# Residual input of the first three projection tiles loaded during the last attention head, into the convolution's buffers

## The chip, the cores and the metric

The kernel runs on one core of a Trainium2 chip. The metric is the device time of one execution in microseconds (us), as the median of several runs; the profile comes from one further execution, taken by the hardware profiler.

## The reference

The input `x` is 1 x 48 x 256 x 256 in float32. Two layers follow, each of the form x + f(group norm of x):

```
# layer 0: attention over 4x4 patches
qkv  = dwconv3x3(einsum('bchw,oc->bohw', gn(x), w_qkv), w_dw)     # 3 x 48 channels
q, k, v = 8 heads of (96, patches); 64 x 64 patches (+ a border of padding)
attn = softmax(normalise(q)^T normalise(k) * temperature)
out  = fold(v attn)                                                # back to 48 x 256 x 256
x    = x + einsum('bchw,oc->bohw', out, w_proj)
# layer 1: three separable mixings of 64 x 64 windows
x    = x + sum_t einsum('bcphqw,wW,hH,cC->bCpHqW', gn(x), Ws[t], Hs[t], Cs[t])
```

The step `x + einsum(out, w_proj)` between the attention and layer 1 is called the projection here; the `x` in it is the residual input.

## The kernel before

The program runs in five stages: statistics and the first pointwise convolution (to 138 us), the depthwise convolution of head 0, eight heads of attention (from 290 us), the projection (3233 to 3385 us) and layer 1.

**Attention.** The loop over heads `h` and sixteen groups `g` of two query blocks is written out by hand under a manual schedule, so instructions stand on each engine in the order of the code. A group runs `scores` (line L337 on TensorE, the exponential L566 on ScalarE), `normalised`, and four calls of `weigh` (`k` = 0 to 3, L595 on TensorE, added up by VectorE in L606 into `oacc`). Queries for group `g + 2` are loaded by SP (L311) as soon as `scores` has read the queries of group `g`, since there are two `qt` buffers. Between these steps heads 0 to 6 also carry the convolution for the head after: strips of the pointwise convolution and the rows of `Depthwise`. Their tiles live in the pool `cv` (`ots`, `xs`, `pad`, `acc`, `o`, `oh` and others), which is opened ahead of the attention and closed with it. In the last head (`more` is false) there is no convolution, and `cv` is not used any more.

**End of a head.** `store(h, m)` turns 512 columns of `oacc` with four transposes (L612), copies them on ScalarE into `oo` (L614, two buffers) and has POOL send them to `os__70` in DRAM as two DMAs (L616). In the last group the stores for `m` = 0 to 5 come at `k` = 1 to 3, and those for `m` = 6 and 7 after the loop.

**Projection.** Eight tiles of 96 partitions (two halves of 48 channels) and 16 rows each. For a tile, SP loads the attention's output `pot` (L740) and the residual input `pxt` (L741), a half at a time, 768 KB a half. TensorE multiplies `pot` by `wp` in four steps (L746, three PSUM buffers), VectorE adds each to `pxt` in place (L753) and takes statistics (L757, eight a tile), and POOL stores the sum to `x1s` in DRAM (L762). The pool `pj` has three buffers each for `pot` and `pxt`; a buffer of `pot` is free when TensorE has read it, one of `pxt` when its store to `x1s` has landed. Here the order on each engine is chosen by the tile scheduler; the order on SP begins with both halves of the first `pxt`, then three of `pot`, then `pxt` and `pot` in turn.

```
ot = pj.tile([P2, KK, NP], F32, name="pot")
xt = pj.tile([P2, RP, W], F32, name="pxt")
for s in range(2):
    ...
    nc.sync.dma_start(out=ot[r], in_=ov[s * (NT // 2 // TP) + t])
    nc.sync.dma_start(out=xt[r], in_=xc[:, y0 : y0 + RP, :])
```

Layer 1 starts when all statistics are there and `x1s` is written: SP loads `lxq` from it (L815).

DMAs of SP and of POOL each rotate over eight semaphores, so the ninth of an engine's DMAs waits for the first one's end.

Of the kernel before, what the change touches and what calls it, by code (L numbers as in the profile page):

```python
# [8 lines left out]
F32 = mybir.dt.float32  # L9
# [7 lines left out]
C = 48  # L17
H = W = 256
HALF = H // 2
P2 = 2 * C  # L20
KS = 4
KK = KS * KS
NH = 8
HD = C * KK // NH
# [9 lines left out]
PX = W // KS  # L34
# [5 lines left out]
TP = 256  # L40
# [5 lines left out]
def conv_preact_kernel(  # L46
# [15 lines left out]
    nc = tc.nc  # L62
    xc = x.rearrange("b c y x -> (b c) y x")
# [34 lines left out]
    for s in range(2):  # L98
        r = slice(s * C, (s + 1) * C)
        for h in range(NH if s == 0 else H0):  # L100
            o = s * M0 + h * HC if h < H0 else (h - H0) * HC
            nc.gpsimd.dma_start(
                out=(wq[r] if h < H0 else wr[0:C])[:, o : o + HC].rearrange("c (z e) -> c z e", z=3),
                in_=w_qkvT.rearrange("c (z h e) -> h c z e", z=3, h=NH)[h],
# [198 lines left out]
    NM = NT // 512  # L303
# [99 lines left out]
    with tc.tile_pool(name="xn", bufs=1) as xnp, tc.tile_pool(name="cst", bufs=1) as cst, tc.tile_pool(  # L403
        name="nps", bufs=2, space=PSUM
# [9 lines left out]
        for i, LR in enumerate(parts):  # L414
            j = sum(parts[:i])
            for s in range(2):
                eng = nc.sync if s == 0 else nc.scalar
                eng.dma_start(
                    out=xr[s * C : (s + 1) * C, j : j + LR, :], in_=xc[:, s * HALF + j : s * HALF + j + LR, :]
# [8 lines left out]
        for g, (w, k) in enumerate(((wq, P2), (wr, C))):  # L428
            m = w.shape[1]
# [48 lines left out]
                nc.sync.dma_start(out=rows, in_=ot[s * M0 : (s + 1) * M0])  # L478

    attention = ExitStack()  # L480
    cv = attention.enter_context(tc.tile_pool(name="cv", bufs=1))
    one = attention.enter_context(tc.tile_pool(name="one", bufs=2, space=PSUM))

    ots = [cv.tile([M1, 4, W + 2], F32, name=f"ot{i}") for i in range(NOT)]
# [5 lines left out]
    with tc.If(nc.values_load(large) > 0):  # L490
# [8 lines left out]
        with tc.tile_pool(name="mk", bufs=NM) as mk, tc.tile_pool(name="mq", bufs=2) as mq, tc.tile_pool(  # L499
            name="mps", bufs=2, space=PSUM  # L500
# [23 lines left out]
    with tc.tile_pool(name="ahead", bufs=2) as ah, tc.tile_pool(name="ae", bufs=3) as ae, tc.tile_pool(  # L524
        name="asm", bufs=6
    ) as asm, tc.tile_pool(name="ao", bufs=1) as ao, tc.tile_pool(name="big", bufs=3, space=PSUM) as big:
        MB = 8
        NK = NB // MB
        NG = NB // G
        keys, queries, values, oaccs = {}, {}, {}, {}  # L530

# [76 lines left out]
        def store(h, m):  # L608

            pt = one.tile([HD, 4, 128], F32, name="pt", tag="one")  # L610
            for i in range(4):
                nc.tensor.transpose(pt[:, i, :], oaccs[h, m // 2][:, m % 2, i * HD : (i + 1) * HD], ident)  # L612
            oo = asm.tile([HD, 512], F32, name="oo", bufs=2)
            nc.scalar.copy(oo, pt.rearrange("p i n -> p (i n)"))  # L614
            for i in range(512 // TP):
                nc.gpsimd.dma_start(  # L616
                    out=os_[m * (512 // TP) + i, h * HD : (h + 1) * HD, :], in_=oo[:, i * TP : (i + 1) * TP]
                )
# [16 lines left out]
        with tc.manual_schedule():  # L635
            load_query(0, 1)
            block = scores(0, 0)
            for h in range(NH):
                more = h + 1 < NH
                rows = {r: Depthwise(h + 1, r) for r in range(CR + 1)} if more else {}  # L640
                for g in range(NG):
                    p, d, n = rows.get(g - 2), rows.get(g - 1), rows.get(g)

                    if h == 0 and 0 < g <= 6:
                        load_value(0, g + 1)
                    if more and CR + 2 <= g < CR + 6:
                        for m in range(2):
                            load_value(h + 1, (g - CR - 2) * 2 + m)
                    if more and CR + 3 <= g < CR + 6:
                        for m in range(2):  # L650
                            load_key(h + 1, (g - CR - 3) * 2 + m)

                    blocks = [normalised(*block)]
                    if p:
                        p.norm()
                        p.root()
                    block = scores(h, g * G + 1)
                    if more and g == NG - 1:
                        load_key(h + 1, 6)
                        load_key(h + 1, 7, nc.gpsimd)  # L660
                    if g + 2 < NG:
                        load_query(h, g + 2)
                    elif more:
                        load_query(h + 1, g + 2 - NG)
                    if p:
                        p.scale()
                    if d:
                        for t in range(1, 4):
                            d.tap(t)
                    second = block  # L670
                    if g + 1 < NG:
                        block = scores(h, (g + 1) * G)
                    elif more:
                        block = scores(h + 1, 0)
                    blocks.append(normalised(*second))
                    if d:
                        for t in range(4, 9):
                            d.tap(t)

                    if g == 0 and rows:  # L680
                        rows[0].load()

                    if h == 0 and 0 < g <= 6:
                        turn(0, g + 1)
                    if more and CR + 2 <= g < CR + 6:
                        for m in range(2):
                            turn(h + 1, (g - CR - 2) * 2 + m)
                    if g == 0 and h > 0:
                        for m in range(6, 8):
                            store(h - 1, m)  # L690
                    if p:
                        p.patches()
                        p.store((2,))
                        p.high()
                    if d:
                        d.square()
                    if n:
                        n.first()
                    for k in range(NK):
                        s = (h * NG + g) * NK + k  # L700
                        weigh(h, g, blocks, k)
                        if k == 0 and d:
                            d.reduce()
                        if k == 0 and p:
                            p.low(nc.gpsimd)
                            p.store((0, 1))
                        if s % 2:
                            for w in strips[s - 1] + strips[s]:
                                w.run(big.tile([128, 2, 512], F32, name="big"))
                            for w in strips[s + 1] + strips[s + 2]:  # L710
                                w.load()
                        elif s:
                            for w in strips[s - 2] + strips[s - 1]:
                                w.store()
                        if k == 2 and g + 1 in rows:
                            rows[g + 1].load()

                        if g == NG - 1 and k > 0:
                            for m in range(2 * k - 2, 2 * k):
                                store(h, m)  # L720
            for m in range(6, 8):
                store(NH - 1, m)
# [1 line left out]


    l1c = ctx.enter_context(tc.tile_pool(name="l1c", bufs=1))
    RP = TP // PX * KS
    NP = TP
    with tc.tile_pool(name="pj", bufs=3) as pj, tc.tile_pool(name="pjs", bufs=1) as pjs, tc.tile_pool(
        name="pps", bufs=3, space=PSUM  # L730
# [2 lines left out]
        ov = os_.rearrange("t (c k) n -> t c k n", k=KK)  # L733
        for t in range(HALF // RP):
            ot = pj.tile([P2, KK, NP], F32, name="pot")
            xt = pj.tile([P2, RP, W], F32, name="pxt")
            for s in range(2):
                r = slice(s * C, (s + 1) * C)
                y0 = s * HALF + t * RP
                nc.sync.dma_start(out=ot[r], in_=ov[s * (NT // 2 // TP) + t])  # L740
                nc.sync.dma_start(out=xt[r], in_=xc[:, y0 : y0 + RP, :])  # L741
            xv = xt.rearrange("p (py ki) (px kj) -> p ki kj py px", ki=KS, kj=KS)
            for ki in range(KS):
                ps = pps.tile([P2, KS, NP], F32, name="pps")
                for i in range(0, KS, 2):
                    nc.tensor.matmul(  # L746
                        ps[:, i : i + 2, :],
                        lhsT=wp,
                        rhs=ot[:, ki * KS + i : ki * KS + i + 2, :],
                        start=True,  # L750
                        stop=True,
                    )
                nc.vector.tensor_add(  # L753
                    xv[:, ki], ps.rearrange("p k (py px) -> p k py px", py=RP // KS), xv[:, ki]
                )
            for i in range(0, RP, 2):
                nc.vector.bn_stats(  # L757
                    st1[:, (t * RP + i) // 2, :], xt[:, i : i + 2, :].rearrange("p a b -> p (a b)")
                )
            for s in range(2):  # L760
                y0 = s * HALF + t * RP
                nc.gpsimd.dma_start(out=x1s[:, y0 : y0 + RP, :], in_=xt[s * C : (s + 1) * C])  # L762
# [14 lines left out]
        for s in range(2):  # L777
            nc.scalar.dma_start(
                out=csn[s * 64 : s * 64 + C].rearrange("c (t d) -> c t d", t=T3), in_=Cs.rearrange("t c d -> c t d")
            )  # L780
            r = slice(s * 64, s * 64 + C)
# [4 lines left out]
        nc.tensor.matmul(pb1, lhsT=mrow, rhs=csn[0:C], start=True, stop=True)  # L786
        cbias = l1c.tile([128, T3 * C], F32, name="cbias")
        nc.vector.tensor_copy(cbias, pb1)


    with tc.tile_pool(name="lx", bufs=3) as lx, tc.tile_pool(name="lz", bufs=2) as lz, tc.tile_pool(
        name="lr", bufs=2
# [109 lines left out]
        with tc.manual_schedule():  # L902
# [4 lines left out]
            late = None  # L907
# [57 lines left out]
```

## Time and profile before

| | us |
|---|---|
| median of 3 runs | 3701.59 |
| lowest, highest | 3696.06, 3705.06 |
| profiled execution, its time | 3698.24 |
| profiled execution, its span | 3696.2 |
| last head's last score matmul ends | 3207.7 |
| first projection matmul (L746) | 3238.9 |
| last statistics of the projection (L757) end | 3379.9 |
| first load of layer 1 (L815) issued | 3384.7 |

The span is the stretch from the first to the last instruction of the profiled execution; what lies around it makes its time 2.0 us longer. The page divides the span into 40 slices of 92.4 us and gives a digit for each engine's busy tenths. Waits name the engine and line that waited, what ended the wait, then the sum in us, the count and the longest. A table of stretches has the busy time of each engine, the granted TensorE clock, the mean busy share of the sixteen DMA engines (1.00 is all of them busy) and the GB/s they moved.

### The profile page before, as it was taken

How to read it: one execution, taken by the hardware profiler on the slowest of the kernel's cores; microseconds unless marked ns; L12 is line 12 of the kernel's file. 1: busy time of each engine (PE TensorE's matmuls, PEld its weight loads, DVE VectorE, ACT ScalarE, POOL GpSimd, SP SyncE). 2: the span in 40 equal slices, each digit the busy share in tenths (PEclk: the TensorE clock that was granted, in tenths of full speed). 3: DMA queues.
4: the chain of work that ended last, by engine and by line, in shares of the span. 5: the costliest groups of instructions: out<-in, count | busy, mean ns of one | idle time of the engine just before them, and what ended most of it. 6: DMA issues, size and time to landing. Idle time of an engine off the chain costs nothing.

```text
span 3696.2 us, 100318 instructions
## 1 busy us (share of the span) xinstructions
PE 3466.8 (94%) x44252; PEld 2905.8 (79%) x44252; DVE 2139.4 (58%) x3514; ACT 1873.3 (51%) x2747; POOL 542.9 (15%) x628
## 2 busy tenths in 40 slices
PE   2869999999999999999999999999999999855998
PEld 1337777898888898988888989888889888713776
DVE  5454774189628953894399349925982222266654
ACT  0235676566546654665566556655664444300332
POOL 2030111012111211121122112201220000000011
PEclk9989999999999999999999999999999999966999
DMA  7455666533323332333233323332333100299774
GB/s 160 152 133 153 176 170 171 149 96 95 94 79 82 93 89 75 83 90 96 73 92 86 87 73 93 86 87 84 94 79 87 36 19 19 51 248 197 127 138 92
DMA packets 274146, 386.48 MB, mean 105 GB/s; under 512 B 77010, under 2 KB 211522, under 8 KB 269480
## 3 DMA queue, kind: packets, MB, share of 16 engines
q1 hardware_dynamic: 234790, 264.95, 27.4%
q0 software_dynamic: 35424, 106.40, 12.4%
q10 hardware_dynamic: 3490, 8.64, 1.1%
q8 instruction: 350, 5.73, 0.7%
q14 instruction: 92, 0.75, 0.1%
HBM read 234.76 MB, written 144.90 MB: 103 GB/s over the span
## 4 chain that ended last, share of the span: by engine, by line
PE 82%; DMA 6%; DVE 2%; issue 1%; SPq 1%; ACT 1%; ACTq 0%; POOL 0%; POOLq 0%; DVEq 0%
PE big L337 36%; PE big L595 35%; PE pb L863 4%; PE pa L841 2%; PE pc L880 2%; DMA pxt<-in_x_dram 2%; DMA t<-ot 1%; PE big L177 1%; DVE acc L228 1%; PE pt L612 1%; DMA pad<-t 1%; PE pn L247 1%; DMA pot<-os__70 1%; PE pst L549 1%; DMA x1s<-pxt 0%
## 5 line engine op out<-in xcount | busy, mean ns | idle before, releaser
L566 ACT ACTIVATE e<-big,nmx 128x1024 f32<-128x1024 f32 x1024 | 1143.8, 1118 | 875.5 <-PE big L337 613.1
L337 PE MATMUL big<-kt,qt 128*128 128x512 f32 x6144 | 1436.7, 392 | 31.1 <-DMA kt<-qkv 29.0
L595 PEld LDWEIGHTS big<-vn,e 128*64 128x64 f32 x32768 | 1357.0, 137 | 57.2 <-ACT e L566 30.6
L595 PE MATMUL big<-vn,e 128*64 128x96 f32 x32768 | 1387.3, 247 | 6.1 <-DVE oacc L606 2.5
L337 PEld LDWEIGHTS big<-kt,qt 128*128 128x128 f32 x6144 | 1144.6, 188 | 279.6 <-issue 28.8
L606 DVE TENSOR_TENSOR oacc<-big,oacc 128x768 f32<-128x768 f32 x480 | 453.4, 954 | 713.0 <-PE big L595 713.0
L228 DVE SCALAR_TENSOR_TENSOR acc<-pad,dwt,acc 126x1024 f32<-126x1024 f32 x592 | 765.5, 1293 | 39.8 <-ACT acc L209 24.0
L295 POOL DMA_DIRECT2D qkv<-o x72 | 52.8, 734 | 1240.7 <-ACT o L279 1240.7
L579 DVE TENSOR_REDUCE zt<-zs 128x1 f32<-128x4 f32 x256 | 38.4, 150 | 335.1 <-ACT e L566 335.1
L289 POOL TENSOR_TENSOR ol<-o,oh 126x1024 fp32r<-126x1024 f32 x78 | 184.9, 2370 | 311.1 <-DVE ss L243 237.8
L566 ACT ACTIVATION_READ_ACCUMULATOR e<-big,nmx 128x1 f32 x1024 | 196.3, 192 | 0.0
L848 DVE TENSOR_TENSOR lzt<-pa,cbias 128x864 f32<-128x864 f32 (+1 forms) x88 | 137.0, 1628 | 96.4 <-PE pa L841 96.4
L870 ACT COPY lyt<-pb 128x512 f32<-128x512 f32 x144 | 84.5, 587 | 212.4 <-PE pb L863 212.4
L279 ACT COPY o<-acc 126x1024 f32<-126x1024 f32 x74 | 159.1, 2150 | 0.0
L863 PEld LDWEIGHTS pb<-wsb,lzt 128*64 128x64 f32 x2304 | 126.1, 138 | 27.6 <-issue 19.5
L616 POOL DMA_DIRECT2D os__70<-oo x128 | 65.2, 515 | 541.6 <-ACT oo L614 541.3
L863 PE MATMUL pb<-wsb,lzt 128*64 128x128 f32 x2304 | 142.0, 279 | 1.3 <-issue 1.3
L746 PE MATMUL pps<-pot,wp 96*96 96x512 f32 x128 | 79.1, 787 | 61.5 <-DMA pot<-os__70 61.5
L239 ACT ACTIVATE sq<-acc 126x1024 f32<-126x1024 f32 x74 | 78.2, 1057 | 100.7 <-DVE acc L228 100.7
L180 ACT ACTIVATE ot<-big,bias 108x1024 f32<-108x1024 f32 x64 | 68.2, 1111 | 113.1 <-PE big L177 71.4
L209 ACT ACTIVATE acc<-pad,dwt 126x1024 f32<-126x1024 f32 x74 | 84.1, 1137 | 80.6 <-DMA pad<-t 80.6
L746 PEld LDWEIGHTS pps<-pot,wp 96*96 96x96 f32 x128 | 26.9, 219 | 113.3 <-issue 79.0
(124 smaller groups left out, 1977.0 us busy)
## 6 DMA issues: line engine op xcount, KB each, us to landing
pad<-t SPq DMA_DIRECT2D x238, 254.0 KB
t<-ot SPq DMA_DIRECT2D x128, 217.7 KB
qkv<-ol POOLq DMA_DIRECT2D x78, 336.0 KB, 6.1
qkv<-oh POOLq DMA_DIRECT2D x70, 336.0 KB, 5.6
qt<-qkv SPq DMA_DIRECT2D x176, 96.0 KB
xs<-in_x_dram SPq DMA_DIRECT2D x128, 96.0 KB
os__70<-oo POOLq DMA_DIRECT2D x128, 96.0 KB, 2.1
pxt<-in_x_dram SPq DMA_DIRECT2D x16, 768.0 KB
```

The costliest lines, as they stand in the source:

```text
L209: nc.scalar.mul(self.acc, self.pad[:, 0:KS, 0:W], dwt[:, self.h, 0:1])
L228: nc.vector.scalar_tensor_tensor(self.acc, self.pad[:, dy : dy + KS, dx : dx + W], dwt[:, self.h, tap : tap + 1], self.acc, ALU.mult, ALU.add,
L279: nc.scalar.copy(self.o.rearrange("p (a b) x -> p a b x", a=KS), self.acc.rearrange("p a (x b) -> p a b x", b=KS))
L289: eng.tensor_sub(self.ol, self.o, self.oh.bitcast(F32))
L337: nc.tensor.matmul(ps[:, i, :], lhsT=qt[:, r, q0 : q0 + 128], rhs=kts[2 * j + i][:, r // 2, :], start=(r == 0), stop=(r == 2),)
L566: nc.scalar.activation(e[:, j * 1024 : (j + 1) * 1024], ps.rearrange("p a b -> p (a b)"), AF.Exp, bias=nmx[:, b : b + 1], accum_out=zs[:, ...
L595: nc.tensor.matmul(ps[p : p + 64, j // 4, j % 4 * HD : (j % 4 + 1) * HD], lhsT=e[:, mb * 128 + p : mb * 128 + p + 64], rhs=vn, start=(i == 0),
L606: nc.vector.tensor_add(oaccs[h, k], ps[:, :, : 4 * HD], oaccs[h, k])
L746: nc.tensor.matmul(ps[:, i : i + 2, :], lhsT=wp, rhs=ot[:, ki * KS + i : ki * KS + i + 2, :], start=True, stop=True,)
L848: nc.vector.tensor_tensor(zv[:, :, y0 : y0 + n, :], pa[:, :, : n * T3 * C].rearrange("p s (y k) -> p s y k", y=n), cbias.rearrange("p (u v ...
L863: nc.tensor.matmul(pb[s * WS : (s + 1) * WS, i, :], lhsT=zts[u][:, t * C + c + i, :], rhs=wsb[:, t, :], start=True, stop=True,)
L870: nc.scalar.copy(yt[:, t, :], pb.rearrange("p i x -> p (i x)"))
```

## The change

The pool `cv` gets a stack of its own at the other end of the on-chip memory (`side="right"`). At the start of the last head it is closed, and a pool `pe` takes its place with three tiles `xt0` to `xt2` for the residual input of projection tiles 0 to 2, and with one `oo` buffer for the very last store (`m` = 7). In groups 1 to 6 of the last head SP gets four loads a group, each a quarter of a half (48 partitions, 4 rows, 192 KB): two at `k` = 1 and two at `k` = 3. The projection uses these tiles for `t` < 3 and issues loads of `pxt` for the other five alone. With `cv` gone from the low end, the pools of the attention and `pj` move down there.

```diff
     attention = ExitStack()
-    cv = attention.enter_context(tc.tile_pool(name="cv", bufs=1))
+    convolution = ExitStack()
+    cv = convolution.enter_context(tc.tile_pool(name="cv", bufs=1, side="right"))
+    NX = 3
     one = attention.enter_context(tc.tile_pool(name="one", bufs=2, space=PSUM))
...
         NK = NB // MB
+        NLATE = 1
+        RP = TP // PX * KS
...
-            oo = asm.tile([HD, 512], F32, name="oo", bufs=2)
+            late = h == NH - 1 and m >= NM - NLATE
+            oo = (pe if late else asm).tile([HD, 512], F32, name="oo", bufs=NLATE if late else 2)
...
                 for g in range(NG):
                     p, d, n = rows.get(g - 2), rows.get(g - 1), rows.get(g)
 
+                    if not more and g == 0:
+                        convolution.close()
+                        early = ExitStack()
+                        pe = early.enter_context(tc.tile_pool(name="pe", bufs=1, side="right"))
+                        xts = [pe.tile([P2, RP, W], F32, name=f"xt{t}") for t in range(NX)]
...
                         if k == 2 and g + 1 in rows:
                             rows[g + 1].load()
+                        if not more and 0 < g <= 2 * NX and k in (1, 3):
+                            i = (g - 1) * 2 + k // 2
+                            t, y = i // 4, i % 4 * (RP // 4)
+                            for half in range(2):
+                                y0 = half * HALF + t * RP + y
+                                nc.sync.dma_start(
+                                    out=xts[t][half * C : (half + 1) * C, y : y + RP // 4, :],
+                                    in_=xc[:, y0 : y0 + RP // 4, :],
+                                )
...
-    RP = TP // PX * KS
...
-            xt = pj.tile([P2, RP, W], F32, name="pxt")
+            xt = xts[t] if t < NX else pj.tile([P2, RP, W], F32, name="pxt")
             for s in range(2):
                 r = slice(s * C, (s + 1) * C)
                 y0 = s * HALF + t * RP
                 nc.sync.dma_start(out=ot[r], in_=ov[s * (NT // 2 // TP) + t])
-                nc.sync.dma_start(out=xt[r], in_=xc[:, y0 : y0 + RP, :])
+                if t >= NX:
+                    nc.sync.dma_start(out=xt[r], in_=xc[:, y0 : y0 + RP, :])
...
         nc.vector.tensor_copy(cbias, pb1)
+    early.close()
```

## The prediction

> **What bounds the kernel now.** I read the 40 slices of the page first, then busy time by stage, then the waits of SP's queue, then the chain that ended last.
>
> ```profile
> PE   2869999999999999999999999999999999855998
> ...
> DMA  7455666533323332333233323332333100299774
> ```
>
> PE is busy in every slice of the attention. Slices 35 and 36 (3234 to 3419 us) are the projection: PE falls to 5 and the DMA engines go to 9. So two stages with different limits touch at about 3233 us. Busy time of two stretches inside the projection:
>
> ```profile
> core 0: us, PE busy (x) PEld busy (x) DVE busy (x) ACT busy (x) POOL busy (x), PEclk, DMA share, GB/s
> 3233.00:3363.00 130.00, 69.36 (x113) 23.85 (x114) 87.22 (x84) 2.45 (x3) 9.11 (x18) 0.70 1.01 255
> 3276.48:3366.44 89.96, 47.44 (x81) 16.41 (x80) 62.12 (x61) 0.00 (x0) 5.04 (x10) 0.71 1.00 263
> ```
>
> The DMA share is 1.01 over 130 us; no other engine is near full. The second line runs from VectorE's first add of tile 2 to that of tile 7, so five tiles took 89.96 us, 18.0 us each. VectorE needs less for a tile:
>
> ```profile
> L753 DVE TENSOR_TENSOR pxt<-pps,pxt 96x1024 f32<-96x1024 f32 x32 | 61.6, 1981 | 56.3 <-PE pps L746 32.4 <-DMA pxt<-in_x_dram 23.9
> L757 DVE BATCH_NORM_STATS2 st<-pxt 96x6 f32<-96x512 f32 x64 | 38.9, 692 | 0.1
> ```
>
> 4 x 1.98 + 8 x 0.69 = 13.4 us. The projection is bound by bytes: a tile moves two halves each of pot, pxt and x1s, 768 KB (0.786 MB) apiece, 4.72 MB. Before it the attention's tail matters. SP's queue from 3200 to 3390 us waited so:
>
> ```profile
> SPq L741 <- DMA x1s<-pxt: 81.2, 5, 22.4
> ...
> SPq L741 <- DVE vn L585: 42.2, 1, 42.2
> SPq L740 <- DMA os__70<-oo: 21.5, 3, 10.9
> ```
>
> The first pxt pair is released by the last head's vn and goes out at 3210.05 us, then SP stands for the output stores of the last head. The chain gives that piece in order of time (start, us, what):
>
> ```profile
> 3217.24 4.19 DMA os__70<-oo
> ...
> 3222.91 6.54 DMA os__70<-oo
> ...
> 3230.93 2.07 DMA os__70<-oo
> ```
>
> Stores of m = 0, 2 and 4 follow each other, because the two oo buffers come free only when a store has landed. The second half of pot for tile 0 is issued at 3232.41 us, after m = 4's first store, and PE's first projection matmul starts at 3238.89. Thus the first pxt pair lies in front of the projection's clock already; the 130 us hold 29 load halves and some 12 store halves.
>
> **What the Trainium skill says.** "DMA: Bandwidth & Descriptors", section "Issuing engines are not separate DMA queues": DMAs of all issuing engines end on the same 16 engines and interleave. The trace agrees: with SP's loads and POOL's stores both pending, the share is 1.00 and the stage runs at the rate of the sum. Same page, "Anatomy of one DMA": a fixed cost of about 2 us, mostly the receipt. The 2.07 us of m = 4's 96 KB store agrees; 4.19 and 6.54 are the same store with a 768 KB load in the queue. "SBUF — State Buffer", "Door 1: The DMA port swizzle": partitions 0 to 63 reach 8 of 16 ports, measured there at 196 GB/s. The halves here have 48 partitions; 3240 to 3250 us, almost all loads, shows 178 GB/s at a share of 0.95. "SBUF — State Buffer", "two separate sides": a DMA and a compute engine do not share SBUF ports. From 2750 to 2800 us the trace has 103 GB/s beside PE busy for 50.00 of 50 us, so it agrees.
>
> **The change, part by part.**
>
> 1. *Removed from the projection:* six pxt halves (tiles 0 to 2), 4.72 MB. Two of these ran before 3232.41 us beside the stores, so four count: 3.15 MB. Price of one: SP's queue in the window 3200 to 3390 took
>
> ```profile
> q1 hardware_dynamic: 3405, 25.86, 61.3%
> q0 software_dynamic: 1792, 14.16, 23.4%
> ```
>
> 61.3% of 190 us for 25.86 MB, 222 GB/s: 3.54 us a half, 14.2 us for four. By the stage's mean of 255 GB/s it is 3.15 / 0.255 = 12.3 us. I take the middle, **13.5 us**; ends 12.3 and 14.2.
>
> 2. *Is the freed DMA time filled?* SP now issues the five pot halves left of tiles 0 to 2 at once; 5 x 3.54 = 17.7 us of loads from about 3232 us. pot of tile 3 waits for PE to have read tile 0 (3238.89 + 10.55 = 3249.4 us before), about when that queue is empty. Then pot and pxt of tile 3 (14.2 us) with x1s of tile 0 (about 4.8) hold the engines to 3268; PE is through with tile 1 by about 3261, so tile 4 queues behind. VectorE, with x there and pot at hand, does tiles 0 to 2 from 3242.8 in 40 us, to 3283, and tile 3 has landed. From tile 6 on it waits for loads as before. pxt of tiles 3 to 5 finds buffers never used, so the 81.2 us of waiting on x1s shrinks to two tiles. No hole: cost 0, covered by a queue filled ahead; 0 to 5 us if loads alone go at the 320 GB/s of some stretches and PE is then late.
>
> 3. *The store chain before the projection.* The pxt pair no longer runs from 3210 to 3220 us, so m = 0's store should take 2.1 us and not 4.19. oo of m = 2 then starts when its transposes end (PE at 3218.98, 0.5 us) and that store lands, 3219.7 and not 3221.53: **1.8 us**. The 6.54 stays, since pot's first half is released by the same store and still sits ahead. If that went too, oo of m = 4 could start at 3223.9 and not 3229.55: 5.6 us. If the store is as slow without pxt: 0. The private buffer for m = 7 takes away its wait on m = 5's store (3237.15 to about 3231); nobody waits for m = 7 before tile 6: 0 gained, 0 lost.
>
> 4. *Added to the last head:* 24 loads of 192 KB on SP, four after each group's queries, in groups 1 to 6. They follow `load_query(h, g + 2)` and stand before that of the next group, which waits for PE anyway:
>
> ```profile
> SPq L311 <- PE big L337: 228.8, 13, 18.9
> ```
>
> 13 waits of 17.6 us in the last head. Four issues (about 0.43 us each) and 0.79 MB at 178 to 222 GB/s are 3.5 to 4.4 us, inside 17.6. A group lasts 21.9 us, so they add 36 GB/s to some 20; heads 0 to 6 carry 75 to 100 with PE full. Cost 0, covered by SP's wait; 0 to 6 us is the range. The first load needs the convolution's buffers, last used in head 6, group 11, some 100 us earlier.
>
> 5. *Moved addresses.* The convolution's pool goes to the far end and everything else down. PE's order is the same in both kernels. VectorE does gm2 later, ScalarE asks for the small csn loads just before the first oo (about 1 us of issue, in the 6.9 us it waits for PE there), POOL's first memset of the ots waits for the last store of the first pointwise stage, as it already did (13.93 us idle to 138.81). 0 each; nothing in the trace prices an address, and I put plus or minus 2 us on it.
>
> Sum: 13.5 + 1.8 = **15.3 us** less. The profiled execution took 3698.24 us, 2.0 more than its span of 3696.2, and becomes 3682.9. The median of the three runs is 3.35 us above it, so the forecast for a median is **3686 us**. What is late next is still the loads, 16 pot and 10 pxt halves with all of x1s.
>
> **Rivals.**
>
> A. *Part of it is given back.* With three pot buffers, tiles 3 to 5 can be asked for only as PE goes on, and PE follows VectorE. For: SP issues pot before pxt of a tile, and one waiting pot holds the pxt behind it. Against: step 2, in which VectorE is ahead of the loads only by a few us. Holes of 5 to 9 us leave 6 to 10 us: 3691 to 3696.
>
> B. *Nothing.* Stores and receipts, not load bytes, set the 18.0 us. For: 255 to 263 GB/s in the mix against 178 in loads alone shows that the price of a load depends on what is beside it. Against: both readings in step 1. About 3700.
>
> C. *Slower.* The added loads make the queries late in the last head. The place is the SP queue between one group's queries and the next; it decides from the point where four loads take more than the 17.6 us of spare, that is under 45 GB/s. Each group over it stalls PE by the excess; at 5 us in six groups it is 30 - 15 = 15 slower, 3717; break-even is 2.6 us a group. Against: the heads with more traffic and a full PE.
>
> D. *More.* The store chain falls by all of its 5.6 us and loads cost 14.2: 19.8, or up to 24 with a faster start: 3677 to 3682.
>
> That the loads do not go where the change says is ruled out by SP's instruction order: four stand after the queries of each of six groups.
>
> **How the numbers follow.** Forecast (12 to 19 us less) 0.72, A 0.15, B 0.03, C 0.05, D 0.05. A measurement of this kernel can tell about 0.3%, 11 us, from no change. Of the forecast 0.04 may fall inside that by scatter (the three runs spread 9 us). Faster: 0.68 + 0.05, rounded to 0.74; same: 0.04 + 0.15 + 0.03, 0.21; slower 0.05. The likeliest case alone is 3682 to 3690; the range takes D below and A above, 3677 to 3697, and leaves C and B out.
>
> **What would show it.** Right: DMA share still about 1.0 from 3233 us on; VectorE without a wait for pxt in tiles 0 to 2; the projection's last bn_stats (3379.9 us now) ending near 3364.5; PE 50 of 50 us in the last head, same start of the projection within 2 us. Step 3 is wrong if the first os stores still take 4 us. Step 2 is wrong if the DMA share has holes near 3250 or 3285. The forecast falls if PE idles in the last head or if 18.0 us a tile stays while fewer bytes move.

## The result, and the profile after

| | before | changed |
|---|---|---|
| median of the runs beside each other, us | 3704.13 (5 runs, 3696.06 to 3705.06) | 3683.15 (5 runs, 3676.71 to 3683.47) |
| profiled execution, time and span, us | 3698.24, 3696.2 | 3683.34, 3681.6 |

The ratio is 0.9942, with a 95% interval of 0.9927 to 0.9956: 16 to 27 us less. A second comparison (among the experiments) gave 0.9955 (0.9941 to 0.9969), 11 to 22 us less. The forecast was 3686 us, 15.3 us less. In medians the two comparisons gave 21.0 and 14.2 us less.

The two profiled spans differ by only 14.7 us, because executions of the same code differ in head 0. At its end the profiled execution of the change is 7.1 us behind that of before, and two further ones of the same code are 2.7 and 10.3 us behind. All are behind, but there is one profile of before, and its time is among the shorter of its runs, so whether the change costs anything in head 0 stays open. From there the offset falls slowly, and it stays at 6.45 to 6.47 us through the last head. From the end of the last exponential to the end of the span, which leaves head 0 out, the trace shows 487.35 us before and 466.19 us after: 21.2 us less.

The 40 slices of the page, as before: slices 35 and 36 hold the projection.

```profile
PE   2869999999999999999999999999999999965998
...
DMA  7455665533323332333233323332333220089774
```

The DMA engines are still at 8 and 9 in the projection's slices (9 and 9 before). In slice 31 (2853 to 2945 us), where the first added loads are, the digit is 2 and was 1.

Busy time by stretch: from tile 0's second pot half to tile 7's first matmul, from VectorE's add of tile 2 to that of tile 7, and 320 us of the last head.

```profile
core 0: us, PE busy (x) PEld busy (x) DVE busy (x) ACT busy (x) POOL busy (x), PEclk, DMA share, GB/s
3239.18:3350.10 110.92, 65.86 (x115) 22.46 (x113) 87.16 (x84) 2.35 (x3) 9.48 (x19) 0.72 1.00 269
3275.46:3353.80 78.34, 45.18 (x73) 15.46 (x74) 62.08 (x61) 0.00 (x0) 5.03 (x10) 0.68 1.01 291
2880.00:3200.00 320.00, 320.00 (x4372) 285.80 (x4372) 75.35 (x177) 146.34 (x244) 4.92 (x10) 1.00 0.14 37
```

The first stretch was 130.29 us and is 110.92. The second, five tiles, was 89.96 us and is 78.34, or 15.7 us a tile. The DMA share is 1.00 and was 1.01, and the rate rose from 255 to 269 GB/s. In the third line PE is busy for all of the 320 us: the added loads, which raised the stage from 20 to 37 GB/s, cost the attention nothing (the table below has its length).

VectorE's rows in the projection, now two forms of the same line (private `xt`, then `pxt`):

```profile
L774 DVE TENSOR_TENSOR pxt<-pps,pxt 96x1024 f32<-96x1024 f32 x20 | 38.3, 1981 | 16.2 <-PE pps L767 9.0 <-DMA pxt<-in_x_dram 7.2
...
L774 DVE TENSOR_TENSOR xt<-pps,xt 96x1024 f32<-96x1024 f32 x12 | 23.2, 1974 | 17.8 <-PE pps L767 17.8
```

The work is the same, 1.98 us an add. The idle time ahead of it fell from 56.3 us to 34.0, and of the 23.9 us for pxt 7.2 are left. What SP's queue waited for from 3200 to 3390 us:

```profile
SPq L760 <- DMA os__70<-oo: 61.6, 2, 53.8
SPq L760 <- PE pps L767: 38.1, 4, 10.8
SPq L762 <- DMA x1s<-pxt: 32.7, 2, 19.9
...
SPq L760 <- PE big L601: 2.8, 1, 2.8
```

The wait of pxt on x1s fell from 81.2 us in five waits to 32.7 in two (tiles 6 and 7). The 53.8 us in the first line are SP standing idle in the attention. The chain ahead of the projection, in order of time:

```profile
3223.99 0.59 ACT oo L621
...
3225.37 2.86 DMA os__70<-oo
...
3230.71 6.88 DMA os__70<-oo
```

The first output store takes 2.86 us and took 4.19; one of the later stores still takes over 6 us. By stretches, taken from landmarks in the trace:

| stretch | before, us | changed, us |
|---|---|---|
| all before the last head, most of it head 0 (offset of VectorE's adds) | | +6.5 |
| last head, from its first group to its last | | 0.0 |
| last `weigh` of the last group (124 matmuls of L595, now L601) | 5.34 | 6.99 |
| first oo copy to first projection matmul | 23.03 | 21.46 |
| first projection matmul to the last bn_stats (VectorE's statistics) | 140.97 | 120.82 |
| layer 1 | | -1.0 |

The longer `weigh` goes with a granted clock of 0.88 from 3210 to 3220 us, where it was 1.00 before. It is not the change's doing: of three executions of the same code two show it, and the third has the clock of 1.00 and no delay.

### The profile page after: what moved, and what is told of

It reads as the page before. It is cut to its first block, busy times and chain, and to the rows that moved or that the text cites. A ratio compares the mean times of both kernels' runs of the same rounds, so it can differ in the third digit from the quotient of the medians.

```text
span 3681.6 us, 100329 instructions
## 1 busy us (share of the span) xinstructions
PE 3468.7 (94%) x44252; PEld 2908.9 (79%) x44252; DVE 2138.6 (58%) x3514; ACT 1873.3 (51%) x2747; POOL 541.7 (15%) x628
## 4 chain that ended last, share of the span: by engine, by line
PE 83%; DMA 3%; issue 3%; DVE 2%; ACT 1%; SPq 0%; POOL 0%; ACTq 0%; POOLq 0%; DVEq 0%
PE big L337 37%; PE big L601 36%; PE pb L885 4%; PE pa L863 2%; PE pc L902 2%; PE big L177 1%; DVE acc L228 1%; PE pt L618 1%; DMA x1s<-pxt 1%; PE pn L247 1%; PE pst L555 1%; DMA kt<-qkv 0%; DMA pxt<-in_x_dram 0%; DMA vt<-qkv 0%; DMA lxq<-x1s 0%
## 5 line engine op out<-in xcount | busy, mean ns | idle before, releaser
L601 PEld LDWEIGHTS big<-vn,e 128*64 128x64 f32 x32768 | 1358.6, 137 | 57.0 <-ACT e L572 30.6
L601 PE MATMUL big<-vn,e 128*64 128x96 f32 x32768 | 1388.9, 247 | 5.9 <-DVE oacc L612 2.6
L243 DVE TENSOR_REDUCE ss<-sq 126x64 f32<-126x1024 f32 x80 | 97.5, 1219 | 27.6 <-ACT sq L239 27.6
```

The source lines that it names most:

```text
L243: nc.vector.tensor_reduce(self.ss, self.sq.rearrange("p a (x b) -> p x a b", b=KS), AX.XY, ALU.add)
L601: nc.tensor.matmul(ps[p : p + 64, j // 4, j % 4 * HD : (j % 4 + 1) * HD], lhsT=e[:, mb * 128 + p : mb * 128 + p + 64], rhs=vn, start=(i == 0),
```

## Experiments

Four readings were to be told apart. Theory L: SP's stream of load halves sets the stage at some 4.4 to 4.5 us a half, and stores ride beside it. Theory S, that of the prediction: all bytes share one pool, 3.1 to 3.5 us a half, whether loaded or stored. Theory B: it is the waits for pxt's buffers. Theory P: a half uses only part of the DMA paths, so two halves at once would go faster. The measure is the time from the issue of tile 0's second pot half to tile 7's first matmul, with the halves that SP issued from that instant on. Kernels that ran only once are not compared by their total time.

| kernel | stretch, us | load halves | us a half |
|---|---|---|---|
| before | 130.3 | 29 | 4.49 |
| one tile ahead | 126.8 | 29 | 4.37 |
| two tiles ahead | 114.9 | 27 | 4.25 |
| two tiles, more `oo` buffers (store chain, below) | 118.0 | 27 | 4.37 |
| the change (three), three profiles | 110.9, 113.7, 109.6 | 25 | 4.44, 4.55, 4.39 |
| own buffers, late loads | 136.6 | 30 | 4.55 |
| three shared buffers | 134.2 | 30 | 4.47 |

**One and two tiles ahead** (`NX = 3` becomes 1 and 2).

> The changed kernel with NX = 1, so only tile 0's residual input is loaded in the last head. I measure the stage from the issue of the second pot half of tile 0 on SP to the first matmul of tile 7: 130.3 us in the kernel before (29 load halves of 768 KB still to come), 110.9 us in the changed one (25 halves). Theory L (the stream of loads sets the stage, stores ride beside it at no cost): 4.47 us a half, so 29 halves again give 129.6. Theory S (all bytes share the 16 DMA engines, as the prediction priced it, 3.1 to 3.5 us a load half and 2.5 to 3.1 a store half): the same bytes as before, 126 to 130. Theory B (waits for x1s to free the three pxt buffers set the stage): one of six such waits is gone, 3 to 6 us less than before, 124 to 127.

> The changed kernel with NX = 2. 27 load halves are left after the start of the stage. L: 27 x 4.47 = 120.7 us. S: 130.3 less 6.2 to 7.1, or from the other end 110.9 plus 6.2 to 7.1: 117 to 124. B: between 115 and 121. With one and three tiles beside it the slope tells: L 9 us a tile, S 6 to 7.

One tile gave 126.8 us with the same 29 halves as before, two gave 114.9 with 27. The first tile ahead is worth almost nothing in this stretch, as its pair had run before it started. Executions of the same code differ by up to 4.1 us here (three profiles of the change; the third is from the run with transfers added after its end), so single steps are not sharp. By means, 30 halves take 135.4 us, 29 take 128.5, 27 take 116.4 and 25 take 111.4: 4.3 to 4.8 us for each half that leaves. The steps look uneven, 6.1 us a half from 29 to 27 and 2.5 from 27 to 25. A likely reason, not tested: in the change VectorE works without a break from 3255 to 3300 us, tiles 0 to 3, so loads no longer set that part of the stage, and a fourth tile loaded early would be worth less still.

**Stores doubled** (POOL writes x of tiles 0 to 2 a second time, to a buffer nobody reads):

```
                 nc.gpsimd.dma_start(out=x1s[...], in_=xt[s * C : (s + 1) * C])
+                if t < NX:
+                    nc.gpsimd.dma_start(out=spare[...], in_=xt[s * C : (s + 1) * C])
```

> The changed kernel with x1s of tiles 0 to 2 stored a second time, to a spare tensor: six more store halves (4.7 MB) from POOL in the middle of the projection; the loads are the same. L: the stage stays at 110.9 us, up to 4 more if POOL's queue makes x1s of tile 3 late for pxt of tile 6. S: six halves at 2.5 to 3.1 us, 126 to 129 us. B: unchanged, 111 to 114.

The stretch took 122.1 us, 11.2 more, between the theories, but not evenly: up to tile 5 nothing moved (tile 5's first matmul 76.9 us after the start, 76.4 in the change), then tile 6 was 14 us late. The queues of the DMA engines from 3260 to 3310 us (packets, MB and share), first in the change and then with the doubled stores:

```profile
q1 hardware_dynamic: 666, 8.09, 64.8%
q0 software_dynamic: 493, 6.21, 35.6%
```

```profile
q1 hardware_dynamic: 662, 8.19, 52.0%
q0 software_dynamic: 663, 8.24, 48.0%
```

SP's loads (q1) moved as much while POOL's stores (q0) moved 2.03 MB more, and the shares add up to 100% in both. The second kernel's stage began 6.2 us earlier, though: from the same point of its stage on (3253.8 to 3303.8 us) it moved 7.91 MB of loads and 7.17 of stores, 0.2 less and 1.0 more than the change. Either way the rate rose (from 287 to 302 or 329 GB/s) at a share of 1.00, so this share did not mean that the engines could carry no more. The delay of tile 6 is a queue: tile 3's x1s stood behind the extra stores on POOL, and pxt of tile 6 waits for it.

```profile
SPq L763 <- DMA x1s<-pxt: 35.7, 1, 35.7
```

**The same stores issued by ScalarE,** to take POOL's queue out of it (`nc.gpsimd` becomes `nc.scalar` in the added line).

> The changed kernel with six more store halves of 768 KB (x of tiles 0 to 2 written a second time, to a buffer nobody reads), this time issued by ScalarE, so that POOL's own x1s stores are not queued behind them. Theory L (loads of 48 partitions go out at 4.4 to 4.5 us a half and stores ride beside them): from tile 0's second pot half to tile 7's first matmul 110 to 114 us, as in the changed kernel (110.9). Theory S (loads and stores share one pool of bytes, 3.1 to 3.5 us a half): 18 to 21 us more, 129 to 132 us. If the earlier try was late only by POOL's queue, pxt of tile 6 goes out near 3314 us and not at 3323.

131.0 us: theory S's number and not theory L's, and still no proof of S. In the trace ScalarE's and SP's DMAs rotate over the same eight semaphores, and not each over its own, so SP's next pot loads had to wait until an extra store had landed:

```profile
SPq L761 <- DMA spare<-xt: 38.0, 4, 25.9
```

From 3255 to 3305 us, SP's queue moved 5.41 MB at a total of 310 GB/s, above the 269 of the changed kernel's stage. The try adds a wait along with the bytes and settles nothing between L and S.

**Own buffers without early loads, and the three shared buffers alone.** In the first, the three private tiles stay, but their loads go out in the projection:

```
-                        if not more and 0 < g <= 2 * NX and k in (1, 3):
+                        if False:
...
+            for t in range(NX):
+                nc.vector.memset(xts[t][:, 0:1, 0:1], 0.0)
...
-                if t >= NX:
-                    nc.sync.dma_start(out=xt[r], in_=xc[...])
+                nc.sync.dma_start(out=xt[r], in_=xc[...])
```

In the second `NX = 0`, all else as in the change.

> The changed kernel with the three extra tiles, but their loads (768 KB a half) stand in the projection and wait for a small memset at the end of the last head, so they have buffers of their own and are not early. 31 load halves after the start of the stage. L: 31 x 4.47 = 138.6 us. S: 130.3 plus two halves at 3.1 to 3.5, 136.5 to 137.3. B: the waits for x1s are gone as in the changed kernel, so 111 to 120.

> The changed kernel with NX = 0: the pools are moved and the last oo has its own buffer, but all residual tiles are loaded in the projection through the three pxt buffers of the kernel before, after pot of the same half. The run with buffers of their own for tiles 0 to 2 and late loads took 136.6 us from the second pot half of tile 0 to the first matmul of tile 7. Theory L (the stream of loads sets the stage): the same 30 or 31 load halves, 134 to 139 us. Theory B (waits for a free pxt buffer): three waits on x1s come back, 3 to 6 us each, 146 us or more. For the moved addresses: the last head ends where a groups' count of 21.9 us puts it, no shift within it.

136.6 us with six buffers for x and 134.2 with three: theory B falls. It is the loads taken out of the stage that count. Both also started late: the time from the first oo copy to tile 0's second pot half was 20.8 and 20.5 us, against 15.2 in the change, since m = 4's store had two load halves ahead of it (own buffers, chain of waits):

```profile
3231.75 12.29 DMA os__70<-oo
```

**The store chain** (`NX = 2`, and `NLATE = 6` in place of 1, so that no oo copy waits for a store).

> The changed kernel with NX = 2 and NLATE = 6: in the last head the copies for m = 2 to 7 have buffers of their own, so none waits for a store to land. Beside it stands the run with NX = 2 and NLATE = 1, where 15.1 us lie between the first oo copy and the issue of the second pot half of tile 0, and 114.9 from there to tile 7. If the two oo buffers set the chain (step 3 of the prediction): the copy of m = 4 follows its transposes, some 8 us after the first, plus 0.9 us of issue and 2.1 to 3 of landing: 11 to 12 us. If pot's first half in the queue sets it: the store of m = 4 takes 6 us as before, 15 us, nothing gained. The stage after it stays at 114.9, within 3.

No gain: 14.8 us from the first oo copy to tile 0's second pot half, and 15.2 with two tiles and two shared oo buffers. m = 4's store took 6.31 us (3231.65 to 3237.96), with its copy no longer late and the load half still ahead of it. The stage after it took 118.0 us, at the edge of what was expected.

**Second halves on ScalarE's queue** (`eng = nc.scalar if s else nc.sync` for pot and pxt).

> The changed kernel with pot and pxt of the second half (partitions 48 to 95) issued by ScalarE's queue and not by SP's; the bytes are the same. Theory P (a load of 48 partitions reaches only some of the SBUF ports, and halves in one queue go one after the other): both halves run at once, a load half falls from 4.47 to 3 to 3.6 us and VectorE (12.6 to 13.4 us a tile) becomes the bound, 95 to 102 us from the start of the stage to tile 7 and not 110.9. Theory S (the 16 DMA engines are full whatever the queue): 108 to 112. A third case: SP's order of pot before pxt no longer holds back the other half, which alone may give 2 to 4 us.

The first matmul came 46.0 us after the last exponential (30.1 in the change), since tile 0's second half was issued later and then ran 17.6 us beside SP's further loads. Then the stage was bound by VectorE, 12.3 to 12.5 us a tile, and took 107.4 us from first matmul to last bn_stats in the place of 120.8. But tile 7 began 134.0 us after the last exponential, and in the change 134.7, so nothing was won. What the loads did is seen before the first matmul, where VectorE did not yet pace the stage: from 3229 to 3257 us, at a share of 1.01, both queues together moved 4.95 MB of loads, 177 GB/s. SP's queue alone moved 3.00 MB from 3240 to 3255 us in the change, 200 GB/s. Two queues carry the stream no faster; theory P, in this form, falls.

**Stores of m = 4 ahead of the first load.** The last group weighs its quarters in the order 0, 2, 1, 3:

```
+                    turns = (0, 2, 1, 3) if not more and g == NG - 1 else range(NK)
-                    for k in range(NK):
-                        s = (h * NG + g) * NK + k
+                    for q, k in enumerate(turns):
+                        s = (h * NG + g) * NK + q
...
-                        if g == NG - 1 and k > 0:
-                            for m in range(2 * k - 2, 2 * k):
+                        if g == NG - 1 and q > 0:
+                            for m in range(2 * turns[q - 1], 2 * turns[q - 1] + 2):
```

> The changed kernel with the last group of the last head weighing its quarters in the order 0, 2, 1, 3, so that the output stores follow as m = 0, 1, 4, 5, 2, 3, 6, 7. What tile 0's second pot half waits for, m = 4's store, is then issued before the first 768 KB load. If what is queued ahead of that store sets the start of the projection: its store takes 2 to 3 us and not 6.3, the time from the first oo copy to tile 0's second pot half falls from 15.2 to 7.5 to 9 us, the stage behind it stays at 110 to 112 us, and the kernel takes 5 to 8 us less than the changed kernel beside it. If the start is hidden by the stream of loads anyway (first pot half out at the same time, tile 7 fixed from there): 0 to 2 us less.

3686.68 us (3677.26 to 3692.42, 6 runs), against 3686.94 for the change beside it: no gain. Tile 7 began 137.2 us after the last exponential, and 137.3 in the change beside it. The store was early as meant, and tile 0's second pot half went out 7.4 us after the first oo copy in the place of 15.2. But now four pot halves go out just ahead of m = 2's two DMAs and two more within a microsecond after them, m = 6's copy needs that store's buffer, and PE's first projection matmul waits for the last copy. Chain of waits, and PE's wait from 3225 to 3255 us:

```profile
3231.52 15.33 DMA os__70<-oo
3246.87 0.04 ACTq L621
3246.91 0.04 issue
3246.95 0.59 ACT oo L621
```

```profile
PE pps L768 <- ACT oo L621: 15.7, 1, 15.7
```

A wait of 6 us was exchanged for one of 15. With buffers of their own for the last copies it might pay; that was not tried.

**The change again,** beside the reordered stores.

> The changed kernel as it is, for a comparison with the reordered stores on the same chip. The load price of 4.5 us and 1.6 us of the store chain give 18 to 20 us less than the kernel before, a ratio of 0.994 to 0.996; head 0 may add up to 7 us to either.

3686.94 us (3683.17 to 3688.27, 6 runs), before 3701.16; ratio 0.9955 (0.9941 to 0.9969), 16.7 us less by the ratio and 14.2 by the medians. The stretch took 113.7 us.

**The price by itself.** After its end, the changed kernel runs groups of transfers, each begun when the one before has landed (shortened):

```
loads(ta, 8)                  # 8 halves of x, SP
gate(ta, ta + tb2)            # VectorE reads what landed, marks what comes next
loads(tb2, 8); stores(ta)     # 8 loads beside 8 stores (POOL)
gate(tb2, ta + tb2)
stores(tb2)                   # 8 stores alone
gate([], tb2 + ta)
4 loads of 96 partitions      # 1.5 MB each
gate(ta, ta + tb2)
for n in (0, 1, 2, 6): loads(tb2, n); one 96 KB store; gate
```

> The changed kernel with transfers alone added after its end, each group begun only when the one before has landed: 8 load halves (48 partitions, 768 KB); 8 load halves beside 8 store halves; 8 store halves; 4 loads of 96 partitions (1.5 MB each); a 96 KB store alone and beside 1, 2 and 6 load halves. The output is the reference's; the time is of no interest, only the groups in the trace. Theory L as the windows of the projection have it (1.96 MB in 10 us for loads alone, 0.2 MB less for each MB stored): 8 loads take 32 to 34 us (4.0 each), beside 8 stores 37 to 41. Theory S (one pool of bytes at 3.1 to 3.5 us a half): 25 to 28 us, and 50 to 56 beside the stores. Loads of 96 partitions: 16 to 18 us for the four if the 48 partitions are what holds a load down, 32 if it is the bytes. The small store: 2 us alone, 6 beside one load, 10 to 12 beside two, over 20 beside six if it waits for all that is ahead of it.

VectorE's one-element operations mark when each group landed (start, duration in us, operation, idle time before and what ended it):

```profile
3723.45 0.15 DVE L956 COPY mk<-ta 96x1 f32<-96x1 f32 x1 [7.43 <-DMA ta<-in_x_dram]
...
3735.31 0.15 DVE L956 COPY mk<-tb 96x1 f32<-96x1 f32 x1 [11.54 <-DMA tb<-in_x_dram]
3746.19 0.15 DVE L956 COPY mk<-tb 96x1 f32<-96x1 f32 x1 [10.73 <-DMA tb<-in_x_dram]
3757.50 0.15 DVE L956 COPY mk<-tb 96x1 f32<-96x1 f32 x1 [11.16 <-DMA tb<-in_x_dram]
3767.38 0.15 DVE L956 COPY mk<-tb 96x1 f32<-96x1 f32 x1 [9.73 <-DMA tb<-in_x_dram]
...
3769.78 0.06 DVE L958 MEMSET ta<- 96x1 f32 x1 [2.01 <-DMA spare<-ta]
...
3798.70 0.06 DVE L958 MEMSET tb<- 96x1 f32 x1 [3.83 <-DMA spare<-tb]
...
3828.86 0.15 DVE L956 COPY mk<-ta 96x1 f32<-96x1 f32 x1 [6.66 <-DMA ta<-spare]
```

| group | issued to landed, us | per 768 KB |
|---|---|---|
| 8 load halves alone | 3685.93 to 3723.45, 37.5 | 4.7 |
| 8 loads beside 8 stores | 3723.77 to 3769.78, 46.0 | 2.9 |
| 8 store halves alone | 3770.16 to 3798.70, 28.5 | 3.6 |
| 4 loads of 96 partitions | 3798.82 to 3828.86, 30.0 | 3.8 |

Stretches from the middle of these groups, by window:

```profile
3700.00:3723.00 23.00, 0.00 (x0) 0.00 (x0) 13.58 (x7) 0.00 (x0) 0.00 (x0) 0.50 0.92 171
3724.00:3767.00 43.00, 0.00 (x0) 0.00 (x0) 0.45 (x3) 0.00 (x0) 4.11 (x8) 0.50 0.97 289
3771.00:3798.00 27.00, 0.00 (x0) 0.00 (x0) 0.18 (x3) 0.00 (x0) 3.24 (x7) 0.50 0.86 233
3800.00:3828.00 28.00, 0.00 (x0) 0.00 (x0) 0.45 (x3) 0.00 (x0) 0.00 (x0) 0.50 0.96 219
```

Loads of 48 partitions alone stop at 171 GB/s with the engines at 0.92, while together with stores the same engines carry 289. Eight loads and eight stores apart sum to 66.0 us and together take 46.0. In the first group VectorE was still clearing the tiles, which let the loads out two at a time until 3699.46 us; the six load halves that end the program, issued within 3 us with VectorE idle, took 28.5 us, 4.7 each again. Where loads are the longer stream, a store half added to them costs (46.0 - 37.5) / 8 = 1.1 us, and a load half taken away is worth up to 4.7. Theory S expected 25 to 28 us and 50 to 56, theory L 32 to 34 and 37 to 41: L has the kind right and is low on both. The windows of the projection are kinder to loads: about 1.95 MB in 10 us when few stores run, 4.0 us a half. Why x alone loads slower than the mix of pot and pxt is not settled. A high share can also come from slow packets. A queue's share times 16 engines times the length of the window, over its packets of 16 KB, gives an estimate of how long one packet holds its engine: 1.42 us for a packet of the loads alone, 1.05 for one of the loads beside stores and 0.71 for one of those stores.

The small store landed after 2.1 us alone, 8.3 beside one load half, 9.7 beside two and 10.0 beside six. But only one half was issued ahead of it in the last two cases, and none in the case before; the others followed it. So the groups don't say what a store does behind several loads.

**pot by 96 partitions.** The groups above suggest a cheaper load. The attention's output is laid out with the two halves of a tile together:

```
-                    out=os_[m * (512 // TP) + i, ...], in_=oo[...]
+                    out=os_[(m % 4 * 2 + i) * 2 + m // 4, ...], in_=oo[...]
...
-        ov = os_.rearrange("t (c k) n -> t c k n", k=KK)
+        ov = os_.rearrange("(t s) (c k) n -> t (s c) k n", s=2, k=KK)
...
-                nc.sync.dma_start(out=ot[r], in_=ov[s * (NT // 2 // TP) + t])
+                if s == 0:
+                    nc.sync.dma_start(out=ot, in_=ov[t])
```

> The changed kernel with the attention's output laid out so that both halves of a tile lie together, and pot loaded by one DMA of 96 partitions (1.5 MB) in the place of two of 48. The same bytes move. If the 48 partitions of a load set its rate: the eight pot loads take about half of their 64 us, the projection becomes bound by VectorE (13.4 us a tile), first projection matmul to last bn_stats falls from 121 to 124 us to 107 to 112, and the kernel takes 10 to 18 us less than the changed kernel. If it is bytes: nothing, or up to 5 us less, since m = 4's store no longer has a pot half ahead of it.

3672.88 us (3668.36 to 3680.41, 6 runs), before 3702.44 beside it; ratio 0.9923 (0.9909 to 0.9937), 23 to 34 us less than before. It has the lowest median here, though it was not run beside the change. First projection matmul to last bn_stats took 109.1 us, as expected of a stage bound by VectorE, with the same bytes moved.

```profile
L775 DVE TENSOR_TENSOR pxt<-pps,pxt 96x1024 f32<-96x1024 f32 x20 | 38.4, 1981 | 5.9 <-DMA pxt<-in_x_dram 5.9
```

The adds of pxt now idle 5.9 us ahead of them, 16.2 in the change. Eight pot loads at 2 x 3.8 us in place of 16 at 4.7 make 14 us less by the group prices; the stage lost 11.7 against the change's first profile and 14.8 against its second. The group prices compare loads from two sources, x and a spare tensor. The stage itself has pot alone on SP's queue from 3240 to 3255 us, from the same tensor; first the change, then pot by 96 partitions:

```profile
3240.00:3255.00 15.00, 9.55 (x15) 3.51 (x16) 4.72 (x4) 1.80 (x3) 2.03 (x4) 0.61 1.04 226
3240.00:3255.00 15.00, 6.13 (x10) 2.29 (x11) 2.34 (x2) 1.97 (x3) 2.03 (x4) 0.58 1.01 264
```

SP's queue moved 3.00 MB in the first and 3.52 in the second, 200 and 235 GB/s. So a load of 1.5 MB into 96 partitions is faster than two of 768 KB into 48, by 1.2 to 1.3 and not by two. What makes it so is not shown: the number of partitions, the size of one transfer and the layout of pot changed together, and in the run with two queues both halves were in flight together and gained nothing.

## Why the prediction was right, and where it was off

**What bounds the kernel.** Right: the loads do. Wrong in the reason given, "bound by bytes". The 1.01 of DMA share was read as a full resource that loads and stores divide. The transfers alone show that stores mostly ride beside the loads (46.0 us together, 66.0 apart), and the doubled stores agree up to tile 5, of which tiles 0 to 3 are paced by VectorE and test little. ScalarE's extra stores leave the question open. In the change the stream of 48-partition loads sets the pace from tile 5 on.

**Step 1, the price of a load half, is the term that was mis-sized.** It put four halves at 13.5 us (12.3 and 14.2 at the ends), 3.1 to 3.5 us each, by dividing time over all bytes. The count of four was right: 29 halves became 25. The stretch lost 19.4 us between the two first profiles, and 16.6 and 20.7 to the other two of the change; over all kernels of the table a half is worth 4.3 to 4.8 us, so four are 17 to 19. The forecast held because its range was wide enough for this. The number was in the prediction's own view: 18.0 us a tile and four load halves a tile are 4.5 us each. And its 178 GB/s for "almost all loads" at a share of 0.95 gives 0.786 / 0.178 = 4.4 us; it was used as an argument for rival B and not as the price.

The Trainium skill's page "SBUF — State Buffer", section "Door 1: The DMA port swizzle", was the lead: partitions 0 to 63 reach half of the ports, 196 GB/s as measured there. The 171 GB/s of loads alone are of that size. But loads into 96 partitions gained 1.2 to 1.3 and not 2, so that ports are the reason is not shown by these runs.

**Step 2.** Right. The DMA share stayed at 1.0, VectorE did tiles 0 to 2 from 3249.24 to 3288.03 us (38.8, where 40 was said) without a wait for pxt, tile 3 had none and tile 4 2.3 us. From tile 5 on it waited for loads, a tile earlier than said (4.83 us at tile 5, behind a PE that waited 8.46 us for pot).

**Step 3.** Right in size, 23.03 - 21.46 = 1.6 us where 1.8 was said, but by another path, so the size is luck. m = 0's store did shrink, to 2.86 us and not to 2.1. m = 4's copy did come early, at 3231.87 us, 7.9 after the first copy where it had been 13.7. But pot's first half, which waits for the last `weigh` and not for a store, was issued at 3231.07, just ahead of m = 4's store, which then took 6.4 us. The copy gained 5.8 us and the store took 4.5 us more. The 5.6 us that step 3 held open were thus not to be had from earlier copies; the store chain with six private buffers (14.8 and 15.2 us) shows it.

**Step 4.** Right: the last head has the same length to 0.02 us, PE at 320 of 320 us.

**Step 5** put the moved addresses at nothing. One effect shows: SP's wait of 2.8 us on the last `weigh` (L601, above) is not in the profile before, where pot's first half waited for a store. That pot now lies where something of the attention lay is the likely reason; it was not tested. This wait is what put pot's first half just ahead of m = 4's store in step 3. The rest lies below what executions differ by.

**The rivals.** A, holes of 5 to 9 us: not there, the share is 0.87 or more in every 5 us from 3240 to 3350. B, stores and receipts set the 18 us: refuted, fewer loads shortened the stage. C, late queries: refuted by step 4's number. D had 19.8 us, which is nearest to the first comparison (21.0 by medians, 21.2 in the trace); the second (14.2 by medians, 16.7 by the ratio) is nearer to the forecast's 15.3. Where D was near, it was for another reason than the one it gave: the loads cost more, and the store chain did not fall.

Of its chances, 0.68 + 0.05 is 0.73 and 0.04 + 0.15 + 0.03 is 0.22, not 0.74 and 0.21.

## What to carry to other kernels

A busy share of 1.0 on the DMA engines does not price a byte: read the price of a transfer from the cadence of the stage, here 18.0 us a tile over four loads of a tile, and count loads and stores apart. Taking loads out of such a stage into one with idle queues pays by about that cadence until another engine sets the pace. Before moving bytes, try one wider load in the place of two, and look at what large loads stand ahead of a small store on the critical path.

## What the runs showed of the hardware

- Loads of x, 768 KB into 48 partitions: 171 GB/s alone; with stores of the same form beside them 289 GB/s in all. Stores alone: 233 GB/s. Loads of 1.5 MB into 96 partitions from a spare tensor: 219 GB/s. Loads of pot: 200 GB/s by 48 partitions and 235 by 96.
- Two issuing queues for the halves moved 177 GB/s of loads of pot and x, no more than one queue did.
- A 96 KB store landed after 2.1 us alone and 8 to 10 us with at most one load half issued ahead of it and one to five after it. In the kernel it took 6.3 us behind one half, 12.3 behind two and 15.3 behind four. One load is enough to make it three to four times as long.
- DMAs issued by ScalarE and by SP share one rotation of eight semaphores in this program, so a transfer on one of them can hold up loads on the other (25.9 us at the longest). POOL's have eight of their own.
